# Three late record reads put ahead of a weight load, one late transposition put ahead of an output product, and an input load put ahead of a weight load

## The chip, the core and the metric

The kernel runs on one core of a Trainium2 chip. The metric is the device time of one execution in microseconds (us); the median of three runs of the kernel before is 632.71 us (632.54 to 634.79).

## What is computed

The input is `x`, 8 sequences of 256 tokens with 256 features, in float32. Four layers each add to it:

```
x = x + L0(x)      # x + attention(16 heads) of a conditioned norm, then a gated MLP of 1024 hidden
x = x + L1(x)      # attention with a mask, output norm, scale and shift from the condition
x = x + L2(x)      # a filter along the sequence and a quaternion rotation
x = x + L3(x)      # a router picks 2 of 8 experts per token; each is a three-layer MLP:

h1 = relu(x @ W1[e] + b1[e])      # 256 -> 512
h2 = relu(h1 @ W2[e] + b2[e])     # 512 -> 512
y  = h2 @ W3[e] + b3[e]           # 512 -> 256
L3(x)[token] = sum over its two experts of  gate weight * y
```

The last layer is computed by tiles: the tokens of one expert are gathered, go through its three products, are scaled by their gate weights and added to the output.

## The kernel before

TensorE (PE) makes every product in float32. A product of one 128x128 block of weights with 256 columns is one matrix instruction in the source and two in the profile (the count beside a group, `x8`, is of those). VectorE (DVE), ScalarE (ACT) and GpSimd (POOL) evict and transform. SyncE (SP) issues most loads; POOL issues the gathers and scatters, whose rows are picked by a list of indices.

**Order of work.** PE executes the matrix instructions in the order of the program's text. DVE and ACT do so too up to the end of the attention layers (`text_order.close()`); after that, and on SP and POOL throughout, a scheduler that models durations places the instructions, and it also decides which of a pool's buffers a new tile takes. `issue_after(i)` holds the instructions in its block behind instruction `i` on their queue. PSUM tiles named `m` come from a pool of three banks (`ps_m`), so a product into a new one waits until the tile that was in its bank has been read.

**The start.** SP issues, in this order: the first half of `x_0`, the conditioning weights `aff_w`, the weights `L0_WkT`, `L0_WqT`, `L0_WvT`, then `x_1`, `x_2`, and four larger weights (lines 605 to 629). `first_norm` (lines 928 to 957, `squares`, `rsqrt`, `xs`) takes the squares of a sequence on ACT, an inverse square root by eleven small DVE instructions (lines 661 to 666), and a scaling `xs_n` on ACT. In the text, and so on DVE, the inverse root for sequence 1 stands ahead of `qz_a` (line 1004), which turns the query product `pq_a` of sequence 0 into the operand of its scores `s_a` (line 1077). PE's order there is `pk_a`, `pq_a`, `pv_a`, `s_a`, then `pt_n` of sequence 1.

**The middle.** After the MLP of a sequence, its result `x2` is transposed on PE (`pt_x`, line 943) and copied to `x2T` by ACT (line 1285), as the operand of the next attention.

**The expert tiles.** `experts(items, ...)` (lines 1626 to 1797) is a generator that runs through a list of tiles. For a tile, `records(n)` reads from SBUF, on SP, where the tile's list of tokens lies (`value_load` of `todo`, line 1640) and loads the list `trec` (line 1642); `fetch(n)` reads which expert it is (line 1648) and loads that expert's weights `w`, 2180 KB, into one of three buffers (`WB = 3`, line 1650); `gather(n)` has POOL gather the tokens' rows, one DMA per 128 tokens or fewer (line 1658); `flip(n)` transposes them on PE (`ptx`, line 1677) and copies them to `xt` on DVE (line 1681); `hidden` makes the first and second product (`ph`, line 1696) with the two halves of each relu on DVE and ACT (lines 1705, 1707); `give` makes the third (`pe`, line 1732), adds the bias on DVE and scales on ACT (`ye`, lines 1745, 1746), and has POOL scatter-add the rows to `out` (line 1748). A scatter waits until the scatters of the tile before it have landed.

There are three lists, one after the other: `s_early` (one tile), `s_sure` (four tiles), and the late list, whose tiles are `a_rest` (256 tokens) and `a_p` (96 to 288 tokens), in the order rest, rest, p3, rest, p1, and so on. The places of the late tiles are only known once the last router choices have been counted and written to the table `slots`. The late list's generator first requests records, weights and gathers (up to its first `yield`), then after a second `yield` turns its first tile (`flip(0)`). The last sure tile calls it once more through `near_end`, ahead of its own `give`:

```
if not within and near_end:
    next(near_end, None)
...
if n > 0:
    yield from give(n - 1, not within and groups == NG)
```

Of the kernel before, what the change touches and what calls it, by code (L numbers as in the profile page):

```python
# [24 lines left out]
NG = B // GB  # L25
# [16 lines left out]
EARLY = -((2 * (T - 2 * TG) - E * (SL - 1)) // -SL)  # L42
SURE = -((2 * (T - TG) - E * (SL - 1)) // -SL)
# [489 lines left out]
def block_kernel(ctx: ExitStack, tc: tile.TileContext, a: dict, out: bass.AP):  # L533
    nc = tc.nc
# [27 lines left out]
    def load(eng, ap, shape, name, dtype=F32, pool=const):  # L562
        t = pool.tile(shape, dtype, tag=name, bufs=1, name=name)
        eng.dma_start(out=t, in_=ap)
        return t

    def load_w(eng, name, rows, cols, pool=const):
        return load(eng, a[name].rearrange("(k p) o -> p k o", p=P), [P, rows // P, cols], name, pool=pool)
# [7 lines left out]
    def load_x(b, engs=(nc.sync,)):  # L576
        xt = pool_a.tile([P, NQ, D], F32, tag="x", bufs=3, name=f"x_{b}")
        n = NQ // len(engs)
        for i, eng in enumerate(engs):
            eng.dma_start(out=xt[:, i * n : (i + 1) * n], in_=x_r[:, b * NQ + i * n : b * NQ + (i + 1) * n, :])  # L580
        return xt
# [25 lines left out]
    xs_in = {0: load_x(0, (nc.sync, nc.scalar))}  # L607
# [12 lines left out]
        nc.sync.dma_start(out=aff_w[:, js, :], in_=a["aff_w"][:, js, :])  # L620
    wk0 = load_w(nc.sync, "L0_WkT", D, D, pool_a)
    wq0 = load_w(nc.sync, "L0_WqT", D, D, pool_a)
    wv0 = load_w(nc.sync, "L0_WvT", D, D, pool_a)
    xs_in[1] = load_x(1)
    xs_in[2] = load_x(2)
    wo0 = load_w(nc.sync, "L0_WoT_turned", D, D, pool_a)
    gate_w = load_w(nc.sync, "gate_wT", D, HID, pool_b)
# [294 lines left out]
    def wt(tag, shape, name, bufs=None):  # L922
        return homes.get(tag, work).tile(shape, F32, tag=tag, bufs=bufs or 2, name=name)

    def bank(name, shape=(P, 2, S)):
        return ps_m.tile(list(shape), F32, tag="m", name=name)
# [12 lines left out]
    def flipped(src, name):  # L939
        pt = bank(f"pt_{name}", (P, KC, S))  # L940
        for k in range(KC):
            for t in range(NQ):
                nc.tensor.transpose(pt[:, k, t * P : (t + 1) * P], src[:, t, k * P : (k + 1) * P], ident)
        return pt
# [18 lines left out]
    def conditioned(xs, b, j, name, eng=(nc.vector, nc.vector), apart=False):  # L963
        if apart:

            pts = [bank(f"pt_{name}_{k}", (P, S)) for k in range(KC)]
            for k in range(KC):
                for t in range(NQ):
                    nc.tensor.transpose(pts[k][:, t * P : (t + 1) * P], xs[:, t, k * P : (k + 1) * P], ident)
        else:  # L970
            pt = flipped(xs, name)
            pts = [pt[:, k, :] for k in range(KC)]
        xT = wt("xT", [P, KC, S], f"xT_{name}", 3)
        for k in range(KC):
            scale, shift = aff[:, j, k, b : b + 1], aff[:, j + 1, k, b : b + 1]
            if eng[k] is nc.scalar:
                nc.scalar.activation(xT[:, k, :], pts[k], AF.Identity, scale=scale, bias=shift)
            else:
                nc.vector.tensor_scalar(xT[:, k, :], pts[k], scale, shift, ALU.mult, ALU.add)
        return xT  # L980
# [176 lines left out]
    def do_deferred():  # L1157
        while deferred:
            for _ in deferred.pop(0):
                pass  # L1160

    def do(parts):
        for _ in parts:
            pass
# [76 lines left out]
    def swiglu(b):  # L1241
        s = state[b]
        do_deferred()
        yT = conditioned(s.pop("xs"), b, 2, f"n2_{b}", (nc.vector, nc.scalar if "xT" in ON_ACT else nc.vector) if b else (nc.scalar, nc.scalar))

        mod = wt("mod", [P, 2 * D], f"mod_{b}")
        nc.sync.dma_start(out=mod, in_=mod_rows[b, :].partition_broadcast(P))
        yield 0.6
        hT = wt("hT", [P, HID // P, S], f"hT_{b}", 1)
        for c in range(0, HID // P, 2):  # L1250
            pg = bank(f"pg_{b}_{c}")
            ph = bank(f"ph_{b}_{c}")
            for ps, w in ((pg, gate_w), (ph, hid_w)):
                for j in range(2):
                    for k in range(KC):
                        o = (c + j) * P
                        nc.tensor.matmul(ps[:, j, :], w[:, k, o : o + P], yT[:, k, :], start=k == 0, stop=k == KC - 1)  # L1257
                if ps is pg:

                    th = wt("th", [P, 2, S], f"th_{b}_{c}")  # L1260
                    nc.scalar.activation(th, pg, AF.Tanh, scale=0.5)  # L1261
                    sg = wt("sg", [P, 2, S], f"sg_{b}_{c}")
                    nc.vector.scalar_tensor_tensor(sg, th, 1.0, pg, ALU.add, ALU.mult)  # L1263
                else:
                    nc.vector.tensor_tensor(hT[:, c : c + 2, :], sg, ph, ALU.mult)
                yield
        pd = bank(f"pd_{b}", (P, NQ, D))
        for t in range(NQ):
            for c in range(HID // P):
                nc.tensor.matmul(  # L1270
                    pd[:, t, :], hT[:, c, t * P : (t + 1) * P], out_w[:, c, :], start=c == 0, stop=c == HID // P - 1
                )
                if c % 4 == 3 and (t, c) != (NQ - 1, HID // P - 1):
                    yield
        x2 = wt("x2", [P, NQ, D], f"x2_{b}", 1)
        nc.vector.scalar_tensor_tensor(x2, pd, 0.5, s.pop("xy"), ALU.mult, ALU.add)
        xs2 = wt("xs2", [P, NQ, D], f"xs2_{b}")
        (nc.vector if "xs2" in ON_DVE else nc.gpsimd).tensor_tensor(
            xs2, x2, mod[:, :D].unsqueeze(1).to_broadcast([P, NQ, D]), ALU.add
        )  # L1280
        s["mod"], s["xs2"] = mod, xs2
        yield
        pt = flipped(x2, f"x2_{b}")
        x2T = wt("xT", [P, KC, S], f"x2T_{b}", 3)
        nc.scalar.copy(x2T, pt)
        yield 0.6
        xg = s["xg"] = wt("xg", [P, NQ, E], f"xg_{b}")
        s["qkv1"] = yield from qkv_last(x2T, b, xg)

    groups = {}  # L1290
# [325 lines left out]
    AHEAD = 3  # L1616
    MOST = max(nq for nq, _ in PIECES)

    def whole(key, n):

        return f"{key}{n}", lambda what: todos[key][0:1, what, n : n + 1], NQ2, P
# [4 lines left out]
    def experts(items, pl, key, groups=NG, near_end=None):  # L1626
# [10 lines left out]
        def records(n):  # L1637
            assert len(placed_) >= groups
            _, at, nq, p = items[n]
            f = nc.sync.value_load(at(1), min_val=0, max_val=DUMMY)  # L1640
            rec = pl.tile("rec", [P, MOST, 4], f"trec_{name_of(n)}", I32)
            nc.sync.dma_start(
                out=rec[0:p, 0:nq, :], in_=slots[bass.ds(f, nq * p), :].rearrange("(q p) c -> p q c", p=p)
            )
            st[n]["rec"] = rec

        def fetch(n):
            e = nc.sync.value_load(items[n][1](0), min_val=0, max_val=E - 1)
            w = pl.weights(f"w_{name_of(n)}")
            nc.sync.dma_start(out=w, in_=a["experts"][bass.ds(e, 1)].rearrange("e p m -> (e p) m"))  # L1650
            st[n]["w"] = w

        def gather(n):
            _, _, nq, p = items[n]
# [103 lines left out]

        def up_to(n, what, do):
            n = min(n, len(items))  # L1760
            for i in range(ahead[what], n):
                do(i)
            ahead[what] = max(ahead[what], n)

        if groups == NG:
            up_to(1, "records", records)
        if groups != NG - 1:
            up_to(1, "fetch", fetch)
        up_to(6, "records", records)
        for i in range(1, AHEAD + 1):  # L1770
# [54 lines left out]
    def left_alone(pl):  # L1825

        mine = Place()
        mine.most = SL

        def tile_(tag, shape, name, dtype=F32):  # L1830
            if tag in ("rec", "xg", "ye"):
                return pl.tile(tag, shape, name, dtype)
            return pl.left.tile(shape, dtype, tag=f"{tag}_left", bufs=1, name=name)

        mine.tile, mine.weights, mine.bank = tile_, pl.weights, pl.bank
        return mine
# [172 lines left out]
    def once(f, *args):  # L2009
        f(*args)  # L2010
        yield
# [92 lines left out]
    for i in range(2, B - 1):  # L2104
# [23 lines left out]
    pl = expert_pools(life_a, life_b2)  # L2128
    others_ = []
    pl.bank = lambda tag, shape, name: ps_m.tile(shape, F32, tag="m", name=name)  # L2130
    first_tile = experts([whole("early", n) for n in range(EARLY)], left_alone(pl), "s", NG - 2)
    sure = experts(
        [whole("sure", n) for n in range(SURE - EARLY)], pl, "s", NG - 1, near_end=(next(others_[0]) for _ in range(1)),
    )

    def later(f):
        yield from f()

    beside |= dict(
        sure=sure, e=first_tile, pl=later(lambda: place_choices(NG - 2)),  # L2140
# [4 lines left out]
    for one in ("q", "rot", "early", "pl", "table"):  # L2145
# [11 lines left out]
        pl=later(lambda: place_choices(NG - 1)),  # L2157
# [76 lines left out]
    with tc.If(either > 0, label="usual"):  # L2234
        with tc.If(tiles_left > 0), ExitStack() as stack:
            pl = expert_pools(stack, stack)
# [90 lines left out]
```

## Time and profile before

| | us |
|---|---|
| median of three runs | 632.71 |
| the profiled execution's own time | 633.01 |
| its span, first to last instruction | 631.3 |
| PE busy | 616.3 |
| DVE, ACT, POOL busy | 359.5, 207.8, 165.8 |
| granted TensorE clock, mean | 0.997 |
| PE busy in the stretch 0 to 15 us | 12.75 |
| PE busy in the stretch 448 to 457 us | 7.71 |
| PE busy in the stretch 457 to 622 us | 165.0 |

The profiled time lies 1.7 us above its span: what lies around the program. Where the text below gives an instruction as "start, duration", both are us from the span's start. In a timeline line, `x8` is a count of merged instructions, and the bracket gives how long the engine had been idle before it and what it waited for. `PEld` is the loading of weights into TensorE, which runs beside its products; SPq is the queue of SP, on which register reads and DMA issues stand.

### The profile page before, as it was taken

The numbers are of one execution on the slowest core, as the hardware profiler recorded it, in microseconds if no ns is written. First come the engines' busy times: TensorE is split into PE (matmuls) and PEld (weight loads), VectorE is DVE, ScalarE is ACT, GpSimd is POOL, SyncE is SP. The second block draws the span as 40 slices with busy tenths as digits, with TensorE's granted clock in tenths as the row PEclk, the third lists the DMA queues.
The fourth block names the chain that finished last, engine by engine and source line by source line (L and its number), as shares of the span: only waits on it lengthen the run. The fifth ranks groups of instructions, "written<-read, shape, count | busy, mean of one in ns | idle before, by whom it ended". The sixth has DMA issues, their size and how long they took to land.

```text
span 631.3 us, 11362 instructions
## 1 busy us (share of the span) xinstructions
PE 616.3 (98%) x4336; PEld 490.6 (78%) x4336; DVE 359.5 (57%) x1186; ACT 207.8 (33%) x382; POOL 165.8 (26%) x289
## 2 busy tenths in 40 slices
PE   8999999999999999999999999999999999999995
PEld 7557777677768776877788867788788898989994
DVE  5664547686688876878889769982222122222221
ACT  3663324534444344445332213222111211212221
POOL 7501200000000610002401362174535343334113
PEclk9999999999999999999999999999999999999998
DMA  8611102002021100010006018654776567659512
GB/s 283 220 34 52 38 6 43 1 19 42 10 76 29 33 2 10 18 67 2 18 12 227 8 44 325 210 160 115 255 187 209 161 226 251 192 173 305 170 20 32
DMA packets 28592, 67.60 MB, mean 107 GB/s; under 512 B 8968, under 2 KB 22064, under 8 KB 26224
## 3 DMA queue, kind: packets, MB, share of 16 engines
q1 hardware_dynamic: 19776, 55.47, 26.5%
q0 software_dynamic: 8464, 11.13, 8.2%
q8 instruction: 36, 0.59, 0.4%
q10 hardware_dynamic: 288, 0.18, 0.1%
q14 instruction: 28, 0.23, 0.1%
HBM read 57.33 MB, written 9.44 MB: 106 GB/s over the span
## 4 chain that ended last, share of the span: by engine, by line
PE 87%; DVE 6%; DMA 2%; ACT 2%; issue 1%; POOL 1%; SPq 0%; POOLq 0%; ACTq 0%
PE ph_a_rest L1696 9%; PE ph_a_p L1696 9%; PE pd L1270 9%; PE ph L1257 9%; PE pg L1257 8%; PE s_a L1077 5%; PE ph_s_sure L1696 4%; PE o_a L1090 4%; PE pq_a L987 4%; PE pe_a_p L1732 3%; PE pe_a_rest L1732 3%; PE py L1149 2%; PE py L1303 2%; PE pv_a L1011 2%; PE pk_a L987 2%; PE pe_s_sure L1732 1%
## 5 line engine op out<-in xcount | busy, mean ns | idle before, releaser
L1079 ACT ACTIVATE pe_a<-s_a 128x2048 f32<-128x2048 f32 x32 | 60.0, 1874 | 54.6 <-PE s_a L1077 51.8
L1257 PE MATMUL ph<-xT_n,hid_wT 128*128 128x256 f32 x256 | 61.6, 383 | 0.0
L1257 PE MATMUL pg<-xT_n,gate_wT 128*128 128x256 f32 x256 | 61.6, 383 | 0.0
L1270 PE MATMUL pd<-out_wT,hT 128*128 128x256 f32 x256 | 59.2, 383 | 0.0
L1270 PEld LDWEIGHTS pd<-out_wT,hT 128*128 128x128 f32 x256 | 47.7, 190 | 11.8 <-issue 4.3
L1257 PEld LDWEIGHTS ph<-xT_n,hid_wT 128*128 128x128 f32 x256 | 47.7, 190 | 11.1 <-issue 2.4
L1257 PEld LDWEIGHTS pg<-xT_n,gate_wT 128*128 128x128 f32 x256 | 47.6, 190 | 10.6 <-issue 1.6
L1202 POOL TENSOR_SCALAR xT_n<-xr,aff 128x256 f32<-128x256 f32 x10 | 5.5, 556 | 173.5 <-DVE rq_v_r L661 54.4
L1696 PE MATMUL ph_a_rest<-h_a_rest,w_a_rest 128*128 128x256 f32 x192 | 42.5, 380 | 0.0
L1707 DVE TENSOR_SCALAR h_a_rest<-ph_a_rest,w_a_rest 128x256 f32<-128x256 f32 x24 | 11.6, 483 | 52.0 <-PE ph_a_rest L1696 49.9
L1696 PE MATMUL ph_a_p<-h_a_p,w_a_p 128*128 128x192 f32 (+3 forms) x224 | 40.2, 338 | 0.0
L1261 ACT ACTIVATE th<-pg 128x512 f32<-128x512 f32 x32 | 19.1, 597 | 63.7 <-PE pg L1257 63.6
L1696 PEld LDWEIGHTS ph_a_rest<-h_a_rest,w_a_rest 128*128 128x128 f32 x192 | 36.0, 190 | 4.6
L1696 PEld LDWEIGHTS ph_a_p<-h_a_p,w_a_p 128*128 128x128 f32 x224 | 37.2, 190 | 1.6
L1077 PE MATMUL s_a<-qz_a,kT_a 32*128 32x512 f32 x256 | 36.5, 639 | 0.9 <-DVE half_c L743 0.6
L1263 DVE SCALAR_TENSOR_TENSOR sg<-th,pg 128x512 f32<-128x512 f32 x32 | 21.8, 681 | 24.0 <-ACT th L1261 23.9
L1456 POOL DMA_INDIRECT slots<-rec,posi x32 | 32.9, 1029 | 9.4 <-POOL rec L1455 7.9
L1707 DVE TENSOR_SCALAR h_a_p<-ph_a_p,w_a_p 128x192 f32<-128x192 f32 (+3 forms) x28 | 12.1, 431 | 40.2 <-PE ph_a_p L1696 37.9
L1748 POOL DMA_INDIRECT out<-ye_a_p,trec_a_p x14 | 20.6, 1475 | 44.0 <-ACT ye_a_p L1746 27.8
L1101 DVE STREAM_TRANSPOSE tu_a<-o_a 128x512 f32<-128x512 f32 x32 | 22.5, 702 | 16.5 <-PE o_a L1090 15.9
L1090 PE MATMUL o_a<-pe_a,va 128*32 128x256 f32 x512 | 30.9, 382 | 0.0
L1705 ACT ACTIVATE h_a_rest<-ph_a_rest,w_a_rest 128x256 f32<-128x256 f32 x24 | 11.4, 474 | 54.8 <-DVE h_a_rest L1707 54.8
(380 smaller groups left out, 1165.3 us busy)
## 6 DMA issues: line engine op xcount, KB each, us to landing
w_a_p<-in_experts SPq DMA_DIRECT2D x7, 2180.0 KB, 9.4
w_a_rest<-in_experts SPq DMA_DIRECT2D x6, 2180.0 KB, 9.5
w_s_sure<-in_experts SPq DMA_DIRECT2D x4, 2180.0 KB, 9.8
w_s_early<-in_experts SPq DMA_DIRECT2D x1, 2180.0 KB, 8.3
mod<-mod_rows SPq DMA_DIRECT2D x8, 256.0 KB, 3.2
tokens<-x SPq DMA_DIRECT2D x4, 512.0 KB, 3.2
out<-x SPq DMA_DIRECT2D x4, 512.0 KB, 4.2
x<-in_x SPq DMA_DIRECT2D x7, 256.0 KB, 2.7
```

Source lines behind the costliest of these rows:

```text
L987: nc.tensor.matmul(pp[:, c, :], w[:, k, c * P : (c + 1) * P], xT[:, k, :], start=k == 0, stop=k == KC - 1)
L1077: nc.tensor.matmul(sc[:, j], kT[r, c, kc * P : (kc + 1) * P], qz[r, c], start=True, stop=True)
L1079: nc.scalar.activation(pe, sc, AF.Exp)
L1090: nc.tensor.matmul(o[32 * i : 32 * i + 32, qd, :], va[:, kc, 8 * c + 4 * qd + i].rearrange("p a d -> p (a d)"), pe[:, 2 * qd + i // 2, i % ...
L1101: nc.vector.transpose(turned.rearrange("p q j a d -> p (q j a d)"), o.rearrange("p q s -> p (q s)"))
L1257: nc.tensor.matmul(ps[:, j, :], w[:, k, o : o + P], yT[:, k, :], start=k == 0, stop=k == KC - 1)
L1263: nc.vector.scalar_tensor_tensor(sg, th, 1.0, pg, ALU.add, ALU.mult)
L1270: nc.tensor.matmul(pd[:, t, :], hT[:, c, t * P : (t + 1) * P], out_w[:, c, :], start=c == 0, stop=c == HID // P - 1)
L1456: sc = nc.gpsimd.indirect_dma_start(out=slots, out_offset=bass.IndirectOffsetOnAxis(ap=posi[:, t : t + 1], axis=0), in_=rec, in_offset=None,)
L1696: nc.tensor.matmul(phs[c - c0][:, 0:many], w[:, o : o + P], src[:, k, 0:many], start=k == 0, stop=k == n_in - 1,)
L1707: relu = nc.vector.tensor_scalar(dst, src_, bias, 0.0, ALU.add, ALU.max)
L1732: mm = nc.tensor.matmul(pos[q][0:p, q % NQ2, :], h2[:, k, q * p : (q + 1) * p], w[:, o : o + D], start=k == 0, stop=k == MC - 1,)
```

## The change

Four edits:

```
@@ the start
     wq0 = load_w(nc.sync, "L0_WqT", D, D, pool_a)
+    xs_in[1] = load_x(1)
     wv0 = load_w(nc.sync, "L0_WvT", D, D, pool_a)
-    xs_in[1] = load_x(1)
     xs_in[2] = load_x(2)
@@ swiglu
-        nc.scalar.copy(x2T, pt)
+        if b == 0:
+            nc.scalar.copy(x2T[:, 0, :], pt[:, 0, :])
+            nc.vector.tensor_copy(x2T[:, 1, :], pt[:, 1, :])
+        else:
+            nc.scalar.copy(x2T, pt)
@@ experts (records, fetch and up_to now return the last DMA that they issue)
         if groups == NG:
-            up_to(1, "records", records)
-        if groups != NG - 1:
+            with tc.issue_after(up_to(AHEAD, "records", records)):
+                w0 = up_to(1, "fetch", fetch)
+            with tc.issue_after(w0):
+                up_to(6, "records", records)
+        elif groups != NG - 1:
             up_to(1, "fetch", fetch)
         up_to(6, "records", records)
@@ the sure tiles
+    def two_of(others_):
+        next(others_[0])
+        next(others_[0])
...
-        [whole("sure", n) for n in range(SURE - EARLY)], pl, "s", NG - 1, near_end=(next(others_[0]) for _ in range(1)),
+        [whole("sure", n) for n in range(SURE - EARLY)], pl, "s", NG - 1, near_end=once(two_of, others_),
```

`AHEAD` is 3 and `groups == NG` holds for the late list (and for a list of rare cases that is not run with this input). `once(f, *args)` is an existing generator that calls `f` and yields. So `x_1` is issued one place earlier on SP; for sequence 0 the copy to `x2T` is made half by ACT and half by DVE; the records of the first three late tiles are requested ahead of the first late weights, and the next three behind them; and the last sure tile advances the late list by two steps, so that `flip(0)` of the late list stands ahead of the last sure tile's `give` on PE.

More of the change, by code (lines that the diff above doesn't have):

```diff
@@ L1641, in records @@
             rec = pl.tile("rec", [P, MOST, 4], f"trec_{name_of(n)}", I32)
-            nc.sync.dma_start(
+            asked_for = nc.sync.dma_start(
                 out=rec[0:p, 0:nq, :], in_=slots[bass.ds(f, nq * p), :].rearrange("(q p) c -> p q c", p=p)
@@ L1645, in records @@
             st[n]["rec"] = rec
+            return asked_for.ins
         def fetch(n):
@@ L1649, in fetch @@
             w = pl.weights(f"w_{name_of(n)}")
-            nc.sync.dma_start(out=w, in_=a["experts"][bass.ds(e, 1)].rearrange("e p m -> (e p) m"))
+            asked_for = nc.sync.dma_start(out=w, in_=a["experts"][bass.ds(e, 1)].rearrange("e p m -> (e p) m"))
             st[n]["w"] = w
+            return asked_for.ins
         def gather(n):
@@ L1760, in up_to @@
             n = min(n, len(items))
+            newest_one = None
             for i in range(ahead[what], n):
-                do(i)
+                newest_one = do(i)
             ahead[what] = max(ahead[what], n)
+            return newest_one
         if groups == NG:
-            up_to(1, "records", records)
-        if groups != NG - 1:
+            with tc.issue_after(up_to(AHEAD, "records", records)):
[3 more added lines that the diff above has]
+        elif groups != NG - 1:
             up_to(1, "fetch", fetch)
```

## Prediction

> **What bounds the kernel now.** I read the busy times first, then the waits of PE, then the timeline around each wait that the edits can touch, and last the table of DMA issues.
>
> ```profile
> PE 616.3 (98%) x4336; PEld 490.6 (78%) x4336; DVE 359.5 (57%) x1186; ACT 207.8 (33%) x382; POOL 165.8 (26%) x289
> ```
>
> PE is busy in 616.3 of 631.3 us, so an edit that leaves PE's instructions as they are can win only out of the 15.0 us in which PE stands, and 7.7 of these lie behind its last product (9.3 us from 622 on, PE busy in 1.6). The waits of PE (total, times, longest, in us) say which of the rest are in reach:
>
> ```profile
> PE ph_a_rest L1696 <- DVE xt_a_rest L1681: 1.0, 1, 1.0
> ...
> PE pv_a L1011 <- ACT x2T L1285: 0.7, 1, 0.7
> ...
> PE s_a L1077 <- DVE half_c L743: 0.6, 1, 0.6
> PE ptx_a_rest L1677 <- DMA xg_a_rest<-tokens,trec_a_rest: 0.3, 1, 0.3
> ```
>
> Each of the four happens once, and each lies where one edit lies. Their sum, 2.6 us, is the size of what is at stake, unless a new wait comes. The late two, on PE:
>
> ```profile
> 447.27 3.67 PE L1732 MATMUL pe_s_sure<-w_s_sure,h_s_sure 128*128 128x256 f32 x16
> 450.78 0.60 PE L1677 MATMUL ptx_a_rest<-ident,xg_a_rest 128*128 128x128 f32 x4
> 452.39 3.72 PE L1696 MATMUL ph_a_rest<-xt_a_rest,w_a_rest 128*128 128x256 f32 x16 [1.01 <-DVE xt_a_rest L1681]
> 455.95 0.27 PE L1677 MATMUL ptx_a_rest<-ident,xg_a_rest 128*128 128x128 f32 x1
> 456.50 0.55 PE L1677 MATMUL ptx_a_rest<-ident,xg_a_rest 128*128 128x128 f32 x3 [0.28 <-DMA xg_a_rest<-tokens,trec_a_rest]
> ```
>
> The turned rows of late tile 0 are needed at once, with no product between, so PE waits for the DVE copy. Tile 1's rows arrive late. Why, SP and POOL show (timeline over all engines):
>
> ```profile
> 432.03 0.99 POOL L1658 DMA_INDIRECT xg_a_rest<-tokens,trec_a_rest  x1 [4.27 <-DMA trec_a_rest<-slots]
> ...
> 436.52 0.34 SPq L1650 DMA_DIRECT2D w_a_rest<-in_experts  x1
> ...
> 437.38 0.38 SPq L1642 DMA_DIRECT2D trec_a_rest<-slots  x1
> ...
> 447.53 1.01 POOL L1658 DMA_INDIRECT xg_a_rest<-tokens,trec_a_rest  x1 [9.40 <-PE ph_s_sure L1696]
> ```
>
> The 4 KB record of tile 1 is issued behind 2180 KB of weights, and POOL's gather stands until 447.53. The table of DMA issues (KB each, median us to landing) has the price of that place:
>
> ```profile
> w_a_rest<-in_experts SPq DMA_DIRECT2D x6, 2180.0 KB, 9.5
> ...
> trec_a_rest<-slots SPq DMA_DIRECT2D x6, 4.0 KB, 7.7
> ...
> trec_s_sure<-slots SPq DMA_DIRECT2D x4, 4.0 KB, 1.7
> ```
>
> A record with no weights ahead lands in 1.7 us, one behind them in 7.7. The bracket at 447.53 names PE's last sure product, but the buffer that this gather fills had been turned by 416 (the copy `xt_s_sure` at 415.91) and the record lands at about 437.4 + 10 = 447.4 (a tile view of these records has 10.5 as its longest): it is the record that POOL waits for.
>
> **Records ahead of the weights.** In the changed program SP reads for record 0, issues it, one read, record 1, two reads, record 2, six reads, then the weights: nine reads, where before it made eleven ahead of the weights and issued the records after them. Before, eleven reads fill 429.87 to 436.52, 0.60 each; a record issue takes 0.38 and a gap of 0.19 (437.38, 437.95). So record 1 goes at 430.5, record 2 at 432.3, and the weights at 429.87 + 9 x 0.60 + 2 x 0.57 = 436.4, where they were at 436.5: cost nothing. The reads ahead of the second weights are 23 in both programs counted from record 0, so these stay at 449.06; they have to be there at 463.8 and took 8.5 to 9.9 us in this stage. POOL then gathers tile 0 (432.0, 433.3), tile 1 (434.6, 435.9) and tile 2 (three, to 441), 1.28 us apart. With the longest landing of such gathers behind weights, 8.6 us in the median for `a_p` and 7.6 for the one on the chain, tile 1 is in SBUF by 444, far ahead of 455. The 0.28 us wait goes; measured by ends it is more: from the end of `ph_a_rest` (456.11) to that of the next 32 products (463.95) are 7.84 us, where four transposes (0.44, as between 450.94 and 451.38) and 32 products (6.92 in the chain) make 7.36. Late next is the relu in front of those products: DVE 0.48 and ACT 0.47 after one another, against 0.44 + 0.65 us of PE work ahead of the operand, so hardly any wait. Gain 0.28 to 0.48, I take 0.4.
>
> What is moved behind: the scatters of sure tile 1 (434.60, 436.54) go from before tile 1's gathers to after five gathers, to about 441, and each later one follows. Nobody on PE waits for them. SP's record read at 453.29 does (its buffer held that sure tile's list), and behind it on SP stand the third late weights, which wait for DVE until 471 anyhow: cover 17 us.
>
> **The weights have new company.** Beside them now run five gathers, 544 rows of 1 KB, 0.56 MB on 2.18 MB. At the same rate the landing of 8.5 to 9.9 us becomes 10.7 to 12.4: 447.1 to 448.8. `ph_a_rest` needs them at 451.3. Cost nothing, with 2.5 us of cover; the far end is in the rivals.
>
> **flip(0) ahead of the last give.** PE ends `ph_s_sure` at 447.44, turns tile 0 (+0.44), makes the sixteen products (+3.45, the chain's length of such a group) to 451.33, and can go on with `ph_a_rest`, which ends 3.45 later at 454.78; before it ended at 456.11. That is 1.33 us; the wait alone is 1.01. The DVE copy (0.68 after two relus) is done by 448.7, beside the products. The rows of tile 0, gathered at 433.3, are there. In the new order the four transposes also lie in front of products that wait for relus (0.19 on PEld at 448.52). The last sure output is 0.4 us later on DVE, and so are the third buffer's weights (452.0 to 452.4, needed at 478). Gain 1.0 to 1.33, I take 1.3.
>
> **x_1 ahead of WvT.** Loads land in the order of issue: WkT 2.49 + 3.8, WqT 3.12 + 5.5, WvT 3.63 + 5.6 = 9.2, `x_1` at about 10.0.
>
> ```profile
> 10.07 0.42 ACT L933 ACTIVATE junk_n<-x 128x256 f32<-128x256 f32 x1 [1.36 <-DMA x<-in_x]
> ...
> 11.15 0.17 DVE L661 TENSOR_SCALAR rq_v_n<-ss_n 128x2 f32<-128x2 f32 x1 [2.00 <-ACT junk_n L933]
> ...
> 13.21 1.41 DVE L1004 TENSOR_SCALAR qz_a<-pq_a,par 128x512 f32<-128x512 f32 x2
> ...
> 14.76 1.14 PE L1077 MATMUL s_a<-qz_a,kT_a 32*128 32x512 f32 x8 [0.61 <-DVE half_c L743]
> ```
>
> ACT and DVE stand idle until `x_1` lands, and the eleven small DVE instructions hold back `qz_a`, which PE waits for. (The bracket names a neighbour; `qz_a` ends at 14.62.) With `x_1` at 9.2 the root is done at 12.5, just as `pq_a` ends (12.42), `qz_a` ends at 13.9, and `s_a` follows `pv_a` (end 14.15) without a stand. WvT then lands at 10.0; its first use is at 12.05. The gain is 0.61 to 0.7 at this place. Down the line the transposed operand (DVE 16.52) cannot move by more than 0.57, since eight small DVE instructions ahead of it wait for a tanh that stays (14.72, behind the eviction of `pv_a`). I take 0.6; the ends are 0 (`x_1` lands no sooner) and 0.7.
>
> **The split copy.** `pv_a` (84.02) waits for the ACT copy only because its bank is that of `pt_x`. In the changed program it takes the bank of `pq_a` instead and waits for `qz_a`, 82.43 + 1.41 = 83.84. So 0.12 of the 0.68 us goes, not all. The halves: ACT 0.38 (a 128x264 copy, L1304), DVE between 0.28 (128x128, L906) and 0.69 (128x512), say 0.45, starting at 83.97 behind another copy; the products that read it come at 86.0.
>
> **Sum.** 0.6 + 0.12 + 1.3 + 0.4 = 2.4 us. The profiled execution's own time is 633.01 (span 631.3), so 630.6; it stands 0.3 above the median, so 630.3 against 632.71. PE is busy in 165.0 of the 165 us from 457 to 622, so what is won ahead of that arrives at the end.
>
> **Rivals.** (1) Weights late, the slower side: the five gathers slow `w_a_rest` until it lands after 451.3, 14.9 us from its issue. If they took every second turn from it while they last and doubled it to 17 to 19.8 us, it would land at 453.4 to 456.2, against 452.39 when PE starts now: 1.0 to 3.8 us lost, less 1.1 won elsewhere: 632.6 to 635.4. For it: from 448 to 457 the DMA engines are 0.87 busy. Against it: that stretch held two weight loads and five gathers at once, and `w_a_rest` took at most 9.9.
> [...]
> (2) The start is bound otherwise (`x_1` lands no sooner, or the gain is swallowed by ACT's exponentials): 630.9. For it: DMA is above 0.8 busy until 25 us. Against: PE's stand is plain, and ACT idles 1.0 and 1.4 us ahead of its first two exponentials.
> (3) The late edits do nothing, because tile 0's rows or the relus are later than I think: only 0.7 us, 632.0. Against: the rows have 14 us.
>
> **How the numbers follow.** The sum 0.72, (2) 0.12, (1) 0.08, (3) 0.08. The forecast's own range is 1.9 to 2.7 us won, 630.0 to 630.8. The range takes in (2), (3) and the lower end of (1), and 0.6 us below for the spread between runs: 629.4 to 632.6. Half a per cent, about what a measurement of this kernel can tell from no change, is 3.2 us: all of the waits together are 2.6. Faster than 629.5 only with that spread's help, 0.12; slower than 635.9 beyond the far end of (1), 0.04; within, 0.84.
>
> **What would show it.** Right: the four waits shrink to under 0.3 us in all; `ph_a_rest` starts 1.3 us after less PE time; the second gather goes at about 434 and not after the first weights land; `s_a` starts near 14.1; `pv_a` still waits some 0.5 us, now for `qz_a`. Wrong: a wait of `ph_a_rest` on a DMA (rival 1), `s_a` still at 14.7 (rival 2), or a new wait of PE between 25 and 430.

## The result, and the profile after

The changed kernel takes 630.87 us in the median of 7 runs (630.79 to 631.14); the kernel before, timed beside it, 632.93 us (632.54 to 634.79). The ratio is 0.9958 with a 95% interval of 0.9948 to 0.9968: 2.1 us won, 0.3 to 0.5 per cent. The forecast was 630.3 us. The profiled execution of the changed kernel took 630.79 us with a span of 629.1, so it stands on the median, and its span is 2.2 us shorter than the one of before.

The busy times and the waits of PE (in all, times, longest, in us):

```profile
PE 616.2 (98%) x4336; PEld 491.9 (78%) x4336; DVE 359.9 (57%) x1187; ACT 207.5 (33%) x382; POOL 165.4 (26%) x289
```

```profile
PE pt_x L943 <- DVE x L1276: 0.8, 1, 0.8
PE s_a L1120 <- ACT qT_a L1061: 0.7, 1, 0.7
PE pv_a L1011 <- DVE shg L918: 0.6, 1, 0.6
PE ph_s_sure L1702 <- DVE h_s_sure L1713: 0.6, 1, 0.6
```

PE does the same work. Of the four waits that the edits touch, three are gone: that for `xt_a_rest`, that for the gathered rows, and that of the first `s_a`. The one of `pv_a` is still there at 0.6. (Its bracket names a neighbour, the copy `shg`; `qz_a`, which ends at 83.51 us, is what `pv_a` waits for, as run four shows.) The late part, on PE:

```profile
446.93 0.60 PE L1683 MATMUL ptx_a_rest<-ident,xg_a_rest 128*128 128x128 f32 x4
447.36 3.62 PE L1738 MATMUL pe_s_sure<-w_s_sure,h_s_sure 128*128 128x256 f32 x16
450.82 3.62 PE L1702 MATMUL ph_a_rest<-xt_a_rest,w_a_rest 128*128 128x256 f32 x16
454.27 0.60 PE L1683 MATMUL ptx_a_rest<-ident,xg_a_rest 128*128 128x128 f32 x4
```

No bracket is left in these lines: the turned rows are copied while PE makes the last sure output, and the transposes of tile 1 run as one group of four. Why its rows are there, SP and POOL show:

```profile
429.10 1.53 SPq L1646 DMA_DIRECT2D trec_a_rest<-slots  x2
432.00 0.34 SPq L1646 DMA_DIRECT2D trec_a_p<-slots  x1
436.15 0.36 SPq L1655 DMA_DIRECT2D w_a_rest<-in_experts  x1
```

```profile
434.22 0.95 POOL L1664 DMA_INDIRECT xg_a_rest<-tokens,trec_a_rest  x1 [0.30 <-issue]
```

Three records go ahead of the weights, and POOL gathers tile 1 from 434.22 instead of 447.53. The weights are requested at 436.15 instead of 436.52, and land 9.7 us after their request in both profiles.

Where the 2.2 us of span come from, by the ends of PE's groups: 0.35 is there before the late part (`ph_s_sure` ends at 447.09 instead of 447.44). The first sixteen `ph_a_rest` end at 454.44 instead of 456.11: 1.67 in all, so 1.32 more, the flip's. The next 32 end at 461.78 instead of 463.95: 2.17 in all, 0.50 more, the records'. From there on nothing changes.

### The profile page after: what moved, and what is told of

It reads as the page before. It is cut to its first block, busy times and chain, and to the rows that moved or that the text cites. A ratio compares the mean times of both kernels' runs of the same rounds, so it can differ in the third digit from the quotient of the medians.

```text
span 629.1 us, 11365 instructions
## 1 busy us (share of the span) xinstructions
PE 616.2 (98%) x4336; PEld 491.9 (78%) x4336; DVE 359.9 (57%) x1187; ACT 207.5 (33%) x382; POOL 165.4 (26%) x289
## 4 chain that ended last, share of the span: by engine, by line
PE 90%; DVE 6%; ACT 2%; POOL 1%; issue 1%; POOLq 0%; ACTq 0%
PE ph_a_rest L1702 10%; PE ph_a_p L1702 9%; PE pd L1270 9%; PE ph L1257 9%; PE pg L1257 9%; PE s_a L1077 6%; PE ph_s_sure L1702 4%; PE o_a L1090 4%; PE pq_a L987 4%; PE pe_a_p L1738 3%; PE pe_a_rest L1738 3%; PE py L1149 2%; PE pv_a L1011 2%; PE pk_a L987 2%; PE py L1307 2%; PE pe_s_sure L1738 2%
## 5 line engine op out<-in xcount | busy, mean ns | idle before, releaser
L1702 PE MATMUL ph_s_sure<-h_s_sure,w_s_sure 128*128 128x256 f32 x128 | 28.6, 382 | 0.6 <-DVE h_s_sure L1713 0.6
```

The lines of the kernel that those rows point to most:

```text
L1702: nc.tensor.matmul(phs[c - c0][:, 0:many], w[:, o : o + P], src[:, k, 0:many], start=k == 0, stop=k == n_in - 1,)
```

## The experiments

Twelve kernels were run, in three sets; within a set all ran on one chip, with the kernel before beside them: 634.05 us there in the first set (20 runs), 633.63 in the second (23), 634.32 in the third (17). So 632.93 was the low side of a kernel that spreads from 632.5 to 636.0. What spreads it is part of what the experiments found. The changed kernel itself ran again beside the second set (630.95 us); the differences of the first set are taken from its 630.87 us.

### One: the second x behind WvT again

```
     wq0 = load_w(nc.sync, "L0_WqT", D, D, pool_a)
-    xs_in[1] = load_x(1)
     wv0 = load_w(nc.sync, "L0_WvT", D, D, pool_a)
+    xs_in[1] = load_x(1)
```

> The changed kernel with one part undone: the second x is requested behind WvT again. In the changed kernel's profile the stretch from pk_a to the first s_a is 0.69 us shorter than before, but pk_a itself began at 9.05 us instead of 8.70. Theory A (the 0.35 us later pk_a is chance: the first 24 keep-busy matmuls stayed slow for one stretch more, whatever the order of the loads): the 0.6 us wait of s_a for DVE returns, the distance pk_a to s_a goes back from 5.37 to about 6.06 us, and over several profiles pk_a begins as often at 8.7 as at 9.05 in either order; time 630.87 + 0.69 = 631.5 us. Rival B (the x request beside the opening loads is what delays them, small_in and with it pk_a): pk_a begins at 8.70 again, and the time rises by 0.35 only, to 631.2 us.

Measured: 631.78 us (631.18 to 632.30), 0.91 above the changed kernel. In its timeline the loads, PE and ACT read:

```profile
8.91 1.99 PE L987 MATMUL pk_a<-xT_n,L_WkT 128*128 128x256 f32 x8
...
15.37 1.14 PE L1077 MATMUL s_a<-qz_a,kT_a 32*128 32x512 f32 x8 [1.01 <-DVE half_c L743]
```

```profile
10.56 0.42 ACT L933 ACTIVATE junk_n<-x 128x256 f32<-128x256 f32 x1 [1.45 <-DMA x<-in_x]
```

ACT waits for the second x until 10.56, and `s_a` starts at 15.37, with a stand of 1.01. `pk_a` did not go back to 8.70. Over the profiles of this study `pk_a` begins at 8.70, 8.91, 8.70, 8.70 and 8.86 with the x behind WvT, and at 9.05, 8.97, 8.86, 8.82, 8.75, 8.54 and 8.75 with it directly ahead: no difference that the order explains (means 8.77 and 8.82). Theory A holds (its 631.5 us was 0.3 too low), B falls. By the trace's record of the clock, the stretch at full clock begins at 6.94 us in the changed kernel's first profile and at 5.76 in that of the kernel before. The program's first 24 matmuls end at 6.98 us in the former, later than in any other profile that has 24 of them (5.81 to 6.91 in the other twelve). `s_a` does separate the two orders: 14.76, 15.37, 15.36, 15.37 and 14.70 behind, 14.38 to 14.49 ahead. The place is worth 0.71 us between the means; the first profile of before, with 14.76, was one of the two in which the x came early.

### Two: the flip behind the last sure output again

```
-        [...], pl, "s", NG - 1, near_end=once(two_of, others_),
+        [...], pl, "s", NG - 1, near_end=(next(others_[0]) for _ in range(1)),
```

> The changed kernel with one part undone: the first late rows are turned behind the last sure output again. Theory A (the flip's 1.3 us is a wait of the matrix engine for the copy xt_a_rest and stands by itself): the wait ph_a_rest for xt_a_rest of about 1.0 us returns, and with the transposes' own second place the end of the first ph_a_rest moves back by 1.32 us: 632.2 us. Rival C (the records' earlier landing would have made most of the flip's room, so that the two share a gain): under 0.7 us, about 631.5 us.

Measured: 632.32 us (632.09 to 633.05), 1.45 above the changed kernel. The waits of PE have the old one back:

```profile
PE ph_a_rest L1702 <- DVE xt_a_rest L1687: 1.0, 1, 1.0
```

Theory A (632.2) holds, rival C (631.5) falls; with the records in their new place the flip is worth its 1.3 us.

### Three: the records behind the weights again

```
         if groups == NG:
-            with tc.issue_after(up_to(AHEAD, "records", records)):
-                w0 = up_to(1, "fetch", fetch)
-            with tc.issue_after(w0):
-                up_to(6, "records", records)
-        elif groups != NG - 1:
+            up_to(1, "records", records)
+        if groups != NG - 1:
             up_to(1, "fetch", fetch)
```

> The changed kernel with one part undone: one late record ahead of the weights and the rest behind them, as in the kernel before; the flip keeps its earlier place. Theory A (terms add): the second tile's gather goes back behind the weights' request, its transposes wait for it again, +0.50 us: 631.4 us. Rival C (with the flip earlier the second tile's transposes come 1.3 us earlier too, so that the wait for its gather grows by that much): 630.87 + 0.50 + 1.32 = 632.7 us, the flip's gain lost at the next wait, and the profile shows a wait of ptx_a_rest for the gather of about 1.6 us. Which one holds decides whether the flip's gain needed the records.

Measured: 635.45 us (635.01 to 635.78 and one of 632.37, 9 runs). That is 4.6 us above the changed kernel, and above the kernel before too (ratio 1.0017, interval 1.0004 to 1.0031). Eight runs took 635.0 us or more. Neither size was expected; theory A, by which the terms simply add, falls. PE, in the profile of this run:

```profile
454.27 0.27 PE L1683 MATMUL ptx_a_rest<-ident,xg_a_rest 128*128 128x128 f32 x1
456.94 0.90 PE L1683 MATMUL ptx_a_rest<-ident,xg_a_rest 128*128 128x128 f32 x3 [2.39 <-DMA xg_a_rest<-tokens,trec_a_rest]
457.63 8.42 PE L1702 MATMUL ph_a_rest<-h_a_rest,w_a_rest 128*128 128x256 f32 x32
```

PE comes to tile 1's transposes at 454.27, as in the changed kernel, and stands 2.39 us for the gather. That is rival C's wait. But then the 32 products take 8.42 us instead of 7.07, and three transposes 0.90 instead of 0.55. The table by stretches (us, busy time and count of PE, PEld, DVE, ACT, POOL, then the granted clock, the share of the DMA engines and GB/s) says why:

```profile
454.50:456.50 2.00, 0.04 (x1) 0.00 (x0) 0.46 (x1) 0.47 (x1) 1.70 (x2) 1.00 1.07 454
456.50:457.00 0.50, 0.06 (x1) 0.07 (x2) 0.00 (x0) 0.00 (x0) 0.50 (x1) 0.94 0.61 238
457.00:457.50 0.50, 0.50 (x3) 0.50 (x4) 0.00 (x0) 0.00 (x0) 0.50 (x1) 0.50 1.71 558
...
459.00:460.00 1.00, 1.00 (x4) 0.82 (x3) 0.00 (x0) 0.00 (x0) 0.80 (x1) 0.50 0.92 327
460.00:460.25 0.25, 0.25 (x2) 0.16 (x2) 0.00 (x0) 0.00 (x0) 0.19 (x1) 0.50 0.57 217
460.25:460.50 0.25, 0.25 (x3) 0.22 (x2) 0.00 (x0) 0.00 (x0) 0.00 (x0) 0.79 0.75 295
```

At the end of the stand the granted clock falls to 0.50 and stays there for 3.4 us (456.94 to 460.36 in the trace's record of the clock). The start of the 32 products is 2.92 us later than in the changed kernel (457.63 for 454.71), and the products last 1.35 longer: 4.27 us, which is the 4.3 us between the spans (633.4 and 629.1).

What such a drop depends on, no run tested. The one run of 632.37 us has a mean granted clock of 0.997, the eight others 0.993 to 0.995, and 3.4 us at half clock is 0.0027 of the mean: by that estimate the ninth run had no drop, and its time is near the 632.7 of rival C.

### Four: x2T copied whole again

```
-        if b == 0:
-            nc.scalar.copy(x2T[:, 0, :], pt[:, 0, :])
-            nc.vector.tensor_copy(x2T[:, 1, :], pt[:, 1, :])
-        else:
-            nc.scalar.copy(x2T, pt)
+        nc.scalar.copy(x2T, pt)
```

> The changed kernel with one part undone: the first sample's x2T is copied whole by ACT again. The trace of the changed kernel shows pv_a beginning 1.31 us after pt_x, 1.33 us before. Theory A (pv_a waits for qz_a, which frees its bank, in either version, so the split wins nothing): 630.87 to 630.9 us, within 0.05. Rival D (the split wins the 0.12 us of the prediction): 631.0 us.

Measured: 631.00 us (630.85 to 631.87). The times alone can't tell 0.02 from 0.12. The timeline can (first this run, then two lines of the changed kernel):

```profile
82.31 0.66 PE L943 MATMUL pt_x<-ident,x 128*128 128x128 f32 x4
83.64 1.99 PE L1011 MATMUL pv_a<-L_WvT,xT_n 128*128 128x256 f32 x8 [0.68 <-ACT x2T L1285]
```

```profile
83.43 0.21 DVE L918 COPY shg<-pshg 128x64 f32<-128x64 f32 x1
83.62 1.38 PEld L1011 LDWEIGHTS pv_a<-L_WvT,xT_n 128*128 128x128 f32 x7 [0.85 <-PE pt_x L943]
```

`pv_a` starts 1.33 us behind `pt_x` with the whole copy, 1.31 with the split one (82.35 and 83.66): the split wins 0.02. In the whole copy's run it starts 0.05 behind the ACT copy (83.59), as in the kernel before, and `qz_a` ended at 83.47: theory A's size is right, and its `qz_a` "in either version" is not. In the changed kernel its weights begin to load at 83.62, before `shg` ends (83.64) and while DVE's half of the copy runs (83.56 to 83.97): that leaves `qz_a`, whose bank it takes.

### Five: the flip alone, on the kernel before

```
-        [...], pl, "s", NG - 1, near_end=(next(others_[0]) for _ in range(1)),
+        [...], pl, "s", NG - 1, near_end=once(two_of, others_),
```

> The kernel before with the earlier turning of the first late rows as its only change. Theory E (the second tile's transposes then come 1.3 us earlier while their gather stays behind the weights' request; PE stands about 2.4 us for it, and behind that stand the granted clock falls to 0.50 for some 3 us, as in the profile of the run with the records put back): that run's 635.45 us plus the 0.9 us that the old place of the second x costs: about 636.3 us, slower than the kernel before by about 2. Rival F (the flip is worth its 1.3 us by itself, and the run with the records put back was slow for another reason): 632.7 us or less.

Measured: 633.65 us (631.73 to 636.25, 12 runs) against 633.63; ratio 1.0000 (0.9987 to 1.0014). The edit worth 1.3 to 1.45 us with the records in place wins nothing that can be told without them (from 0.8 us faster to 0.9 slower). Rival F falls. Theory E was right in kind and wrong in size: the stand is there, and in this profile the granted clock stays at 1.00 behind it:

```profile
455.32 0.27 PE L1677 MATMUL ptx_a_rest<-ident,xg_a_rest 128*128 128x128 f32 x1
457.14 0.55 PE L1677 MATMUL ptx_a_rest<-ident,xg_a_rest 128*128 128x128 f32 x3 [1.55 <-DMA xg_a_rest<-tokens,trec_a_rest]
```

PE comes 1.05 us later than in run three, since in this kernel the second x is late; the stand is 0.84 shorter, the clock stays at 1.00, and the median is 1.8 us below run three's (of another set). So more is won back at the gather than was lost at the start. The runs from 631.73 to 636.25 fit stands of different lengths, but only this one was profiled; their mean clock of 0.996 to 0.998 speaks against a drop in any of them, the run of 636.25 (0.996) included.

### Six: the records alone, on the kernel before

The edit of `experts` from the change, without the other three.

> The kernel before with the three late records ahead of the first late weights as its only change. Theory E (the kernel before owes its spread of 632.7 to 635.4 us to the second tile's gather, which lands beside the weights now sooner, now later, with the clock's drop behind a long stand): the spread shrinks to about 1 us, and the median is that of the run with the flip put back, 632.3, plus 0.9 for the second x: about 633.2 us, 0.9 under a kernel before at 634.05. Rival G (the spread is that of the opening or of the chip, and the records win the 0.4 to 0.5 us read from one profile): the spread stays over 2 us and the median lies 0.5 under that of the kernel before.

Measured: 633.10 us (632.37 to 633.30, 12 runs) against 633.63 (632.46 to 635.56, 23 runs); ratio 0.9988 (0.9979 to 0.9996). The spread shrinks from 3.1 us to 0.9, as theory E has it, and so rival G falls; the level is theory E's 633.2, but 0.53 under the kernel before is G's size and not the 0.9 expected (the interval, 0.25 to 1.3, takes in both). There is no wait for gathered rows among this run's waits. What theory E says of the clock is not borne out: the slowest run of the kernel before in this set, 635.56 us, has a mean clock of 0.997, and the profile with the drop 0.995. What such a slow run loses its time on was never profiled.

### Seven: half of one qz_a on ACT

```
-            if j and "qz" in ON_ACT:
+            if j and name == "a0_3":
                 nc.scalar.activation(qz[:, :, j, :], pq, AF.Copy, scale=par[:, j : j + 1])
```

> The changed kernel with one addition: of the fourth sample's qz_a the second half is scaled by ACT (idle then from 81.8 to 83.1 us) instead of DVE. Theory A (pv_a stands 0.65 us for qz_a, which frees its bank at 83.5, and not for the copies of x2T): qz_a ends near 82.9, pv_a begins right behind pt_x at about 83.0, and the time falls by 0.6 us to 630.3 us. Rival D (pv_a waits for x2T, the split half on DVE): no gain, 630.9 us.

Measured: 630.37 us (630.36 to 630.50), 0.58 under the changed kernel of the same set; ratio to the kernel before 0.9948 (0.9934 to 0.9961).

```profile
82.42 0.66 PE L943 MATMUL pt_x<-ident,x 128*128 128x128 f32 x4
83.10 1.99 PE L1011 MATMUL pv_a<-L_WvT,xT_n 128*128 128x256 f32 x8
```

```profile
82.83 0.21 DVE L918 COPY shg<-pshg 128x64 f32<-128x64 f32 x1
82.95 0.69 ACT L1002 ACTIVATE qz_a<-pq_a,par 128x512 f32<-128x512 f32 x1 [1.93 <-DVE qz_a L1004]
```

`pv_a` follows `pt_x` without a stand, although the two halves of x2T are copied only at 84.33 and 84.72 here: rival D falls, and the copies did not hold it. But theory A's way was not taken either. ACT's half of `qz_a` runs behind DVE's half, to 83.64, and `pv_a` starts at 83.10, before it ends; so it is not in the bank that `qz_a` reads. It is in that of `pshg`, which DVE's copy `shg` frees at 83.04, 0.6 us earlier than in the changed kernel, since `shg` stands behind half a `qz_a` only. The 0.6 us came from DVE's shorter work and another bank.

### Eight: the changed kernel again

> The changed kernel itself, beside the others on one chip. Theory E: 630.9 us within 0.3, with a spread under 1 us, while the kernel before spreads over 2.5 us around 634; ratio 0.995. Over the profiles pk_a begins between 8.7 and 9.05 us in either order of the loads (theory A for the start). Rival G: the changed kernel spreads as the kernel before does.

Measured: 630.95 us (630.82 to 630.99, 5 runs), ratio 0.9956 (0.9942 to 0.9970) to a kernel before at 633.63 that spreads over 3.1 us. The spread of 0.2 us is as theory E has it. Against the whole spread of before the change is worth 2.7 us rather than 2.1.

### Nine: the second x alone, on the kernel before

The two lines of run one, exchanged in the kernel before.

> The kernel before with the second x requested ahead of WvT as its only change. In the profiles so far the first s_a begins at 14.38 to 14.49 us with the x ahead and at 14.76, 15.36, 15.37 and 15.37 with it behind, wherever pk_a began. Theory E (the late part is paced by the second tile's gather, which follows the late records' landing beside the weights, so that PE only stands longer there): of the 0.9 us less than 0.5 comes through, the stand for the gather grows by about as much, and the median lies within 0.5 us of the kernel before, about 633.4 us. Rival H (the gains are independent of each other): 0.9 us under the kernel before of the same chip, about 632.8 us.

Measured: 633.43 us (632.50 to 634.98, 12 runs) against 634.32; ratio 0.9986 (0.9976 to 0.9996), 0.25 to 1.5 us faster. The level is the 633.4 of theory E, but the difference, 0.9, is rival H's, and the interval takes in both: not settled. In the profile `s_a` starts at 14.38, 0.38 ahead of the first profile of before, and PE stands 0.96 us for the gather, 0.68 more: against that profile the stand took the whole gain (spans 631.6 and 631.3).

### Ten: the kernel before again

> The kernel before, for a profile other than the first, whose time (633.01 us) lay near the low end of its runs. Theory E: where the time is about 633.6 us or more, the first s_a begins at about 15.4 us instead of 14.76, or PE stands over 0.28 us for the second tile's gather, or both, and the rest of the trace is as in the first profile. Rival G (the spread comes from elsewhere): these two stretches are as in the first profile and the time is lost somewhere else.

Measured: 632.81 us, one run at the low end again, so it can't show where a run of 634 loses. It shows the other end of the gather's scatter:

```profile
436.37 0.34 SPq L1650 DMA_DIRECT2D w_a_rest<-in_experts  x1
437.22 0.38 SPq L1642 DMA_DIRECT2D trec_a_rest<-slots  x1
```

```profile
446.03 1.01 POOL L1658 DMA_INDIRECT xg_a_rest<-tokens,trec_a_rest  x1 [7.83 <-DMA trec_a_rest<-slots]
```

Requested 0.2 us earlier than in the first profile, the record lets POOL gather 1.5 us earlier, and PE does not stand. Put together, the profiles with the late record (times in us):

| kernel | POOL gathers tile 1 | PE is ready for its rows | its rows are there | stand |
|---|---|---|---|---|
| before, again | 446.03 | 456.17 | earlier | 0 |
| before | 447.53 | 456.22 | 456.50 | 0.28 |
| second x alone | 447.79 | 455.85 | 456.82 | 0.96 |
| flip alone | 447.93 | 455.59 | 457.14 | 1.55 |
| all but the records | 447.79 | 454.54 | 456.94 | 2.39 |

(Ready: the end of the group's first transposition. There: the start of the other three.) In four of the five the rows come at 456.5 to 457.1, however early PE is. That is the floor under every edit ahead of it, and of the four edits only the records lift it.

### Eleven: the second x ahead of WqT too

On top of run seven:

```
+    xs_in[1] = load_x(1)
     wq0 = load_w(nc.sync, "L0_WqT", D, D, pool_a)
-    xs_in[1] = load_x(1)
```

> The kernel with half of one qz_a on ACT, and the second x requested ahead of WqT too. Its first s_a begins 14.49 us after the start, 0.5 us after PE was free. Theory A (s_a is set by the landing of the second x, 5.6 us behind its request at 3.6): the request moves 0.5 us earlier, ACT's junk_n begins right behind xT_n, and the time falls by 0.1 to 0.5 us, to 629.9 to 630.3 us; WqT lands near 9.4 us, still ahead of pq_a at 10.4. Rival B (the loads share one path, and the x moved up delays WkT and WqT by as much): pk_a or pq_a waits, and the time is 630.4 us or more.

Measured: 630.32 us (630.21 to 630.73), 0.05 under run seven, which ran in another set: no gain that can be told. The steps were as expected (ACT's `junk_n` at 8.85, right behind `xT_n`, and no stand of `s_a`), but PE itself came 0.27 later (`pk_a` at 8.81 for 8.54), so `s_a` starts at 14.38, 0.11 ahead of run seven's 14.49. Theory A's 0.1 to 0.5 us was a miss; rival B's 630.4 us or more did not come either.

### Twelve: twenty keep-busy matmuls for twenty-four

On top of run eleven:

```
-        keep_busy(12)
+        keep_busy(10)
```

> The kernel of the run beside it (half of one qz_a on ACT, second x ahead of WqT) with 20 instead of 24 of the first keep-busy matmuls. Theory A (paff follows these matmuls, whose end differs by 0.5 us from profile to profile with the clock's warming up): paff waits for aff_w instead, pk_a begins at 8.5 to 8.7, and the time is the same as beside it or up to 0.3 us less. Rival I (the matmuls left out warm the clock): the granted clock rises later, the opening's matmuls run longer and the time is 0.3 us or more above that of the run beside it.

Measured: 630.54 us (630.25 to 631.91), against 630.32: no gain, and not the 0.3 us of rival I either, so undecided. `paff` starts at 6.13 instead of 6.38, but takes 0.91 us for its eight instead of 0.64, and `pk_a` (8.74 for 8.81) waits for `xs_n` and its transposition. The twenty matmuls take 4.64 us here, 0.232 each, and the twenty-four of run eleven 4.96, 0.207 each, so they ran slower here, as rival I has it. But 24 of them took anywhere from 4.32 to 5.49 us over the profiles: one profile each can't tell.

## Why the prediction was right, and where not

**The flip, 1.3 us.** Right: 1.32 by the ends of the groups, 1.45 in the medians of run two. What the step left out is its condition. It costed the flip beside the records as if each stood alone; by run five it wins nothing that can be told without them. In the sum this did no harm, because both were in the change.

**The records, 0.4 us.** Right for the profile it was worked out from (0.50), with the gather at 434.22 for a forecast of 434 and the scatters at 440.38 for 441. The term was mis-sized in what it stands for: taken out of the changed kernel it costs 4.6 us, since the flip and the second x bring PE to the gather 1.7 us earlier, and behind the stand of 2.39 us that followed the granted clock was 0.50 for 3.4 us and PE's next two groups took 1.7 us longer (0.90 for 0.55, 8.42 for 7.07). The "how the numbers follow" part had no case with such a stand. It also took the profile's 0.28 us wait for the rule, while the kernel before spreads over 3 us, and the records alone take that to 0.9.

**The new company of the weights.** The step "at the same rate the landing of 8.5 to 9.9 us becomes 10.7 to 12.4" failed: with five gathers beside them the first late weights took 9.7 us, as in the first profile of before. They are there at 445.9, for a use at 450.82. Rival 1 is ruled out, and with it the doubled landing of 17 to 19.8 us. That the gathers would double it was a supposition; how the DMA engines divided their time between the two, no run here shows. How much more company the weights would stand was not tried. "These stay at 449.06" failed too: the second weights went at 447.31. Before, two of the record issues behind the weights took 1.31 and 1.15 us, now 0.33 to 0.39 each, which is 1.7 us by the timeline. But the second profile of before, with the records behind the weights, has 0.45 and 0.37 there, so the edit need not be the cause; it cost and won nothing.

**The second x, 0.6 us.** The mechanism was right (ACT's `junk_n` at 9.24 in place of 10.07), the size depends on the profile: 0.34 for the start of `s_a` against the first profile of before, 0.71 between the means over twelve profiles, 0.91 in the medians of run one. `s_a` came at 14.42 and not "near 14.1": `pk_a` was 0.35 late, which run one showed to be scatter. Rival 2 is ruled out.

**The split copy, 0.12 us.** Wrong, 0.02. The step took the end of `qz_a`, 83.84, as the start of `pv_a`. But PE starts 0.15 us behind `qz_a` (83.51 to 83.66), while it had started 0.05 behind ACT's copy (83.97 to 84.02). That difference took the gain. It is not one between DVE and ACT: behind DVE's `xt_a_rest` PE started after 0.06 (452.33 to 452.39). Behind `qz_a`, here and ahead of the first `s_a` (14.62 to 14.76), the trace has a wait of its own on PE's queue, 0.05 us long, ahead of the weight load (83.55 to 83.60 here), which the views leave out. That `pv_a` would then wait for `qz_a`, and still some 0.5 us (0.65), was right; it also means that the sign "under 0.3 us in all" for the four waits could not come true, and it didn't.

**Sum.** By the prediction's own base, one profile against the other, 2.4 us were forecast and 2.2 measured: 0.35 for 0.72 at the start and the split copy, 1.32 for 1.3, 0.50 for 0.4. Of the 0.57 us between 630.3 and 630.87 that is 0.2; 0.3 more is the amount by which the profiled run of before stood over the three-run median, which was taken off as if the changed kernel had it too, although its runs hardly spread; the last 0.08 is the changed kernel's median over its profiled run. The 630.87 lies just above the narrow range of 630.0 to 630.8, and inside the wide one. Luck has a part in the 2.1 us: both the 632.71 and the 632.93 are low draws of a kernel whose larger sets have 633.63 to 634.32. Rival 3 (the late edits do nothing) is ruled out by runs two and three.

## What to carry to other kernels

Before pricing an edit that brings an engine to a wait earlier, find when the thing it waits for arrives; if that is fixed by another queue, the gain ends there, as at the rows that came at 457.14 us in run five. In such a place a small load that unlocks a gather belongs ahead of the large one beside it: here that let the gather start at 434.22 us instead of 447.53. Price a wait of PE not by its length alone: behind one of 2.39 us the clock was 0.50 and the next groups took 1.7 us longer, behind one of 1.55 us it stayed at 1.00; what decides between the two, no run shows. And when a kernel's runs spread by more than the edit is worth, one profile is one draw; read the same two lines in several before you take their difference for a term.

## What the runs showed of the hardware

A stand of PE of 2.39 us was followed by a granted clock of 0.50 for 3.4 us; after one of 1.55 us it stayed at 1.00. A 4 KB record requested 0.85 us behind 2180 KB of weights on the same queue let its gather start 8.8 us (437.22 to 446.03) or 10.2 us (437.38 to 447.53) after its request in two executions of the same kernel; with three such records ahead of the weights instead, the runs of one set spread over 0.9 us, those of the kernel before over 3.1. And the first 24 matmuls of the program ended at 6.06 to 6.46 us in the five profiles with the second x behind WvT, and at 5.81 to 6.98 in the eight with it ahead.
